# One score product per lent bank, and softmax exponentials handled four heads at a time on GpSimd

## The chip, the cores and the metric

The kernel runs on one core of a Trainium2 chip. The metric is the device time of one execution in microseconds; the median of several runs counts. One further execution is recorded by the hardware profiler; its trace is what the readings below come from. Engine names are those of the profile: PE is TensorE (PEld its weight loads), DVE is VectorE, ACT is ScalarE, POOL is GpSimd, SP is SyncE, which issues most of the transfers.

## The reference

A conditioned transformer block on `x` of shape 2 x 2048 x 512, with 16 heads of 32 and a hidden layer of 2048:

```python
mod = silu(condition) @ Wada + bada
sh_a, sc_a, gt_a, sh_m, sc_m, gt_m = split(mod, 6, axis=1)
xm = layernorm(x, g1, be1) * (1 + sc_a) + sh_a
x = x + gt_a * attention(xm, Wqkv, Wproj, bproj)      # causal, softmax over keys
xm = layernorm(x, g2, be2) * (1 + sc_m) + sh_m
h = gelu(xm @ W1 + b1)                                # exact gelu
x = x + gt_m * (h @ W2 + b2)
```

In `attention`, `scores = q k^T / sqrt(32)`, entries above the diagonal are minus infinity, and the softmax subtracts the largest score of each row.

## The kernel before, in words

The two batch rows go one after the other: projections to queries, keys and values (`Qkv`), attention (`attention_phase`), output projection (`project_phase`), and the next row's projections. The hidden layer for both rows comes last. The dense products use a seven-product scheme for 2 x 2 blocks. Nearly every matmul goes through one helper, so its line is L206 for all of them, and the tiles tell them apart.

Attention is cut into 16 units per batch row: a group `c` of four heads (`HC = 4`) and a block `i` of 512 queries, in the order i = 0, 1, 2, 3 for the first group and 0, 2, 1, 3 for the others. A unit runs steps over tiles of 128 keys: 4 i full steps, then the tile on the diagonal, a step with two tiles (384 and 128 queries wide) and a last one of 256 queries. In a step (`scores_t`) PE writes for each of the four heads the negated row maximum into an `st` bank of PSUM (the fold matmul, `st<-fold,sel`) and adds the transposed scores (`st<-qst,kst`); ACT takes the exponential into a tile `e` (L630); on the last three steps of the unit GpSimd zeroes the masked part of `e` (`affine_select`, L636). Two steps later (`LAG = 2`) PE multiplies `e` by the values (`o<-e,vv`).

The sums of the exponentials are formed in chains of four full steps: GpSimd adds the second tile to the first, the third and the fourth to that (`begin_chain`, `add_to`, L658), and PE reduces the chain over partitions four steps after the last add (`sm<-ee,ones`). The diagonal step's tile joins the last chain; the unit's last steps are summed by PE directly. In the last unit of a batch row VectorE does the adds in place of GpSimd. Tiles rotate: 16 `e` tiles are four steps of four heads, 8 `ee` tiles two chains.

The row maxima of a unit must be known before it begins. `Row` computes them up to three units ahead (`AHEAD = 3`): PE computes scores untransposed (`s<-kst,qst`) into a bank, and VectorE reduces them, a full-width product of 512 keys by a maximum (L500), one on the diagonal by a masked maximum (L495, followed by a read of the accumulator). Products on the diagonal are only 128, 256, 384 or 512 wide; `banks_of` puts two of them into one bank (a pair: 128 with 384, or 256 with 256), all others stand alone. When a unit's list is done, `split` reduces the maxima and splits them into three 16-bit parts (L517 to L521, with the last bank as scratch), and `rows` turns them into the fold operand (L561, L565).

PSUM's eight banks: four `st`, two `s` (`ps_sp`), one `o`, one `sm`. A planner (`count`, `due`) gives each attention step a number of score banks, `n`. With `n` of 3 or more, two of them are computed in `s` after the first two heads' exponentials; after the heads, one takes a borrowed `st` bank (`score(1, st_bank)`), and the fourth takes `s` again:

```python
if n >= 3:
    row.score(1, st_bank)
    row.score(min(n, HC) - 3)
```

`score` takes the list `todo` from its head, in the order of `banks_of`, whether the next entry is a pair or a single. The same function also runs during `Qkv`, between the projections' products, without a borrowed bank. Every instruction of `mm` and `act` keeps its place in the program's order on its engine.

Of the kernel before, what the change touches and what calls it, by code (L numbers as in the profile page):

```python
# [27 lines left out]
def dit_block_kernel(  # L28
# [45 lines left out]
    MTT = MT // P  # L74
    NG = T // MT
    LAG = 2
    E_BUFS = 16
    EE_BUFS = 8
    AHEAD = 3

    const = ctx.enter_context(tc.tile_pool(name="const", bufs=1))
# [213 lines left out]
    class Row:  # L295
# [234 lines left out]
                n += 1  # L530
            return n

        def score(self, n, borrow=None):

            for k in range(n):
                if borrow and k % 2 == 0:
                    s = borrow()  # L540
                else:
                    s = ps_sp.tile([P, QB], F32, tag="s", name="s")
                item = self.todo.pop(0)
                u = item[0]
                if self.mx is None:
                    self.mx = bp.tile(
                        [P, HC * TQ, units[u][1] + 1], F32, tag="mx", name="mx", bufs=3
                    )
                self.bank(*item, s)
                if not self.todo or self.todo[0][0] != u:  # L550
                    self.split(u, self.mx, s)
                    self.mx = None
                    self.at += 1
# [26 lines left out]
    def attention_phase(row):  # L580
        b, vv, kst, qst = row.b, row.vv, row.kst, row.qst
        with pool(f"att{b}") as ap, pool(
# [6 lines left out]
            def scores_t(u, step, n):  # L589

                def st_bank():

                    n_bank[0] += u == len(units) - 1
                    if n_bank[0] % 6 >= HC:
                        return ps_sp.tile([P, QB], F32, tag="s", name="st")
                    return ps_stp.tile([P, QB], F32, tag="st", name="st")

                c, i = units[u]
                tiles = steps_of[u][step]
                q0 = tiles[0][1]
                w = sum(QB - q for _, q in tiles)
                sts, es = [], []  # L610
                for h in range(HC):
                    g = slice(h * HD, (h + 1) * HD)
                    st = st_bank()
                    mm(
                        st[:, :w], sel[g, :], fold[u % 2][g, q0 : q0 + w],
                        start=True, stop=False,
                    )
                    sts.append(st)
                for h in range(HC):
                    at = 0  # L620
                    for j, q in tiles:
                        mm(
                            sts[h][:, at : at + QB - q],
                            kst[c, j // TQ][:, h, j % TQ * P : (j % TQ + 1) * P],
                            qst[u][:, h, q:],
                            start=False, stop=at + QB - q == w,
                        )
                        at += QB - q
                    e = ap.tile([P, QB], F32, tag="e", name="e", bufs=E_BUFS)
                    act(nc.scalar.activation(e[:, :w], sts[h][:, :w], AF.Exp))  # L630
                    if tiles[0][0] >= i * TQ:

                        d = e.rearrange("p (t k) -> p t k", k=P)[:, 0 : TQ : TQ - 1, :]
                        d = d[:, : len(tiles), :]
                        act(
                            nc.gpsimd.affine_select(  # L636
                                d, d, pattern=[[0, len(tiles)], [1, P]],
                                compare_op=ALU.is_ge, fill=0.0,
                                base=0, channel_multiplier=-1,
                            )  # L640
                        )
                    es.append(e)
                    if h < 2 and n >= 3 or h >= HC - n and n < 3:
                        row.score(1)
                if n >= 3:
                    row.score(1, st_bank)
                    row.score(min(n, HC) - 3)
                return es, max(0, n - HC)

            def new_sums():  # L650
                return [
                    ap.tile([P, QB], F32, tag="ee", name="ee", bufs=EE_BUFS)
                    for _ in range(HC)
                ]

            def add(u, h, dst, x, y):
                engine = nc.vector if u == len(units) - 1 else nc.gpsimd
                act(engine.tensor_tensor(dst, x, y, ALU.add))  # L658

            def add_to(u, chain, es):  # L660
                for h in range(HC):
                    add(u, h, chain[h], chain[h], es[h])

            def begin_chain(u, es0, es1):
                chain = new_sums()
                for h in range(HC):
                    add(u, h, chain[h], es0[h], es1[h])
                return chain

            def products(dst, lhs, es, q0, at, first, last):  # L670
                for h in range(HC):
                    mm(
                        dst[h * HD : (h + 1) * HD, q0:], lhs(h),
                        es[h][:, at : at + QB - q0], start=first, stop=last,
                    )

            def finish(u, o, sm):
# [1359 lines left out]
```

## Time and profile before

| | |
|---|---|
| median of 3 runs | 2343.66 us (2343.58 to 2346.75) |
| the profiled execution | 2339.57 us, span 2337.8 us, granted clock 0.997 |
| busy: PE, DVE, ACT, POOL | 2272.5, 1432.3, 1007.9, 1119.2 us |
| attention of the first row, 214 to 748 us | PE 520.4, DVE 358.4, ACT 302.4, POOL 436.5 us busy |
| attention of the second row, 990 to 1518 us | PE 515.7, DVE 354.8, ACT 298.0, POOL 430.9 us busy |

A busy time counts the modelled run of an instruction, and matmuls overlap in the pipeline. A row of a timeline reads: start, length, engine, line, operation, output<-inputs, shapes, how many in a row, and in brackets the idle time of the engine ahead of it with what ended it. A row of the waits reads: who waited for whom, microseconds in all, times, the longest. A row of a group ends in busy time, the mean of one in nanoseconds, and the idle time ahead of the group with what ended it. Line numbers are those of the kernel before.

### The profile page before, as it was taken

What the parts mean: (1) busy time and instruction counts of PE and PEld (TensorE: products, weight loads), DVE (VectorE), ACT (ScalarE), POOL (GpSimd) and SP (SyncE); (2) the same over time, 40 slices, a digit from 0 to 9 for tenths busy, and PEclk for the clock granted to TensorE, in tenths of its full rate; (3) what the DMA queues carried; (4) which work ended last, traced back from release to release, by engine and by line L of the source; (5) the groups of instructions that cost most, each with busy time, mean ns of one, the idle gap of its engine ahead of it and who ended that gap; (6) DMA issues with size and microseconds to landing.
All of it is one profiled execution on the core that took longest, in us unless ns stands there. A gap on an engine that the chain in (4) does not pass through costs nothing.

```text
span 2337.8 us, 34364 instructions
## 1 busy us (share of the span) xinstructions
PE 2272.5 (97%) x12033; PEld 1376.1 (59%) x12033; DVE 1432.3 (61%) x3025; ACT 1007.9 (43%) x1952; POOL 1119.2 (48%) x1261
## 2 busy tenths in 40 slices
PE   7999999999999999999999999999999999999998
PEld 5787445455544588754545554344585486487477
DVE  4677766767657657777576766562473383375356
ACT  4434555555555243355555555603323322332320
POOL 7153997988893692289888898450000000000000
PEclk9999999999999999999999999999999999999999
DMA  9887132231223796622324113263354254353433
GB/s 303 272 277 185 33 86 65 64 83 46 91 100 116 260 307 222 167 60 67 75 64 100 42 42 133 97 229 108 107 176 154 84 176 145 116 162 126 141 120 131
DMA packets 160518, 311.64 MB, mean 133 GB/s; under 512 B 16544, under 2 KB 48844, under 8 KB 158552
## 3 DMA queue, kind: packets, MB, share of 16 engines
q1 hardware_dynamic: 155488, 285.53, 40.5%
q0 software_dynamic: 4480, 23.36, 2.6%
q8 instruction: 95, 1.56, 0.3%
q14 instruction: 79, 0.65, 0.1%
q10 hardware_dynamic: 376, 0.55, 0.1%
HBM read 229.95 MB, written 87.29 MB: 136 GB/s over the span
## 4 chain that ended last, share of the span: by engine, by line
PE 83%; DVE 6%; POOL 6%; issue 2%; DMA 2%; ACT 1%; SPq 0%; DVEq 0%; POOLq 0%; ACTq 0%
PE ps_a L206 24%; PE st L206 15%; PE ps_b L206 12%; PE o L206 9%; PE s L206 7%; PE ps_c L206 6%; POOL ee L658 5%; PE sm L206 4%; PE ps_o L206 3%; DVE junk L495 2%; PE ps_xt L214 1%; DVE mx L500 1%; POOL e L636 1%; ACT e L630 1%; PE ps_o L214 1%
## 5 line engine op out<-in xcount | busy, mean ns | idle before, releaser
L630 ACT ACTIVATE e<-st 128x512 f32<-128x512 f32 (+1 forms) x1152 | 574.5, 578 | 413.6 <-PE st L206 380.0
L500 DVE TENSOR_REDUCE mx<-s 128x1 f32<-128x512 f32 x608 | 406.2, 686 | 223.1 <-PE s L206 221.8
L658 POOL TENSOR_TENSOR ee<-ee,e 128x512 f32<-128x512 f32 x424 | 529.1, 1293 | 3.5 <-ACT e L630 3.3
L206 PE MATMUL st<-qst,kst 128*128 128x512 f32 (+3 forms) x1280 | 410.6, 386 | 0.0
L206 PE MATMUL s<-kst,qst 128*128 128x512 f32 (+3 forms) x994 | 375.3, 402 | 6.0 <-DVE mx L500 3.1
L206 PE MATMUL ps_a<-sum,w 128*128 128x256 f32 (+1 forms) x1088 | 346.6, 454 | 0.0
L206 PE MATMUL o<-e,vv 128*32 128x512 f32 (+3 forms) x2560 | 310.2, 539 | 6.9 <-POOL e L636 6.7
L206 PEld LDWEIGHTS st<-qst,kst 128*128 128x128 f32 x1280 | 227.8, 188 | 117.6 <-issue 88.3
L206 PEld LDWEIGHTS ps_a<-sum,w 128*128 128x128 f32 x1088 | 206.4, 190 | 109.7 <-issue 91.3
L658 POOL TENSOR_TENSOR ee<-e 128x512 f32<-128x512 f32 x168 | 210.3, 1288 | 102.3 <-ACT e L630 100.6
L495 DVE CUSTOM_DVE_ANT_0 junk<-s,causal 128x128 bf16<-128x128 f32 (+3 forms) x386 | 188.5, 488 | 92.4 <-PE s L206 85.0
L206 PEld LDWEIGHTS s<-kst,qst 128*128 128x128 f32 x994 | 185.7, 188 | 55.5 <-DVE mx L500 20.5
L636 POOL TENSOR_SCALAR_AFFINE_SELECT e<-e 128x128 f32<-128x128 f32 (+1 forms) x384 | 123.6, 362 | 73.1 <-ACT e L630 70.8
L206 PEld LDWEIGHTS <-sel 32*128 32x128 bf16 x1152 | 29.5, 91 | 199.7 <-issue 199.7
L1616 DVE TENSOR_TENSOR h<-c,ps_b 128x512 f32<-128x512 f32 x32 | 22.0, 688 | 202.0 <-PE ps_b L206 202.0
L206 PE MATMUL st<-fold,sel 32*128 32x512 bf16 (+1 forms) x1152 | 127.9, 372 | 13.5 <-DVE mx L495 6.4
L206 PEld LDWEIGHTS o<-e,vv 128*32 128x32 f32 x2560 | 65.3, 108 | 112.4 <-issue 72.8
L1790 ACT ACTIVATE h<-h,cols 128x512 f32<-128x512 f32 x96 | 69.3, 722 | 120.5 <-DVE h L1616 120.5
L206 PE MATMUL ps_b<-sum,w 128*128 128x256 f32 (+1 forms) x384 | 120.6, 450 | 0.0
L500 DVE TENSOR_REDUCE mx<-st 128x1 f32<-128x512 f32 x160 | 109.4, 684 | 2.4 <-PE st L206 0.6
L985 POOL TENSOR_TENSOR lo<-lo,hi 128x512 fp32r<-128x512 f32 x32 | 40.7, 1274 | 130.4 <-ACT hi L983 124.1
L206 PE MATMUL st<-kst,qst 128*128 128x512 f32 (+3 forms) x286 | 98.0, 370 | 0.0
(210 smaller groups left out, 3113.9 us busy)
## 6 DMA issues: line engine op xcount, KB each, us to landing
kst<-k SPq DMA_DIRECT2D x128, 256.0 KB
qst<-q SPq DMA_DIRECT2D x128, 256.0 KB
w<-w1d SPq DMA_DIRECT2D x32, 896.0 KB
w<-w2d SPq DMA_DIRECT2D x28, 1024.0 KB
w<-w2d SPq DMA_DIRECT2D x28, 768.0 KB
q<-hi SPq DMA_DIRECT2D x32, 256.0 KB
q<-lo SPq DMA_DIRECT2D x32, 256.0 KB
k<-hi SPq DMA_DIRECT2D x32, 256.0 KB
```

The source lines that it names most:

```text
L206: return tc.keep_in_program_order(nc.tensor.matmul(*args, **kw))
L214: return tc.keep_in_program_order(nc.tensor.transpose(dst, src, ident[:n, :n]))
L495: nc.vector.tensor_tensor_reduce(junk[:, :w], x, causal[:, QB - w :], 1.0, MASKED, ALU.add, ALU.max, m,)
L500: nc.vector.tensor_reduce(m, x, axis=AX.X, op=ALU.max)
L630: act(nc.scalar.activation(e[:, :w], sts[h][:, :w], AF.Exp))
L636: nc.gpsimd.affine_select(d, d, pattern=[[0, len(tiles)], [1, P]], compare_op=ALU.is_ge, fill=0.0, base=0, channel_multiplier=-1,)
L658: act(engine.tensor_tensor(dst, x, y, ALU.add))
L985: engine.tensor_tensor(lo, d, hi.bitcast(F32), ALU.subtract)
L1616: act(nc.vector.tensor_tensor(dst, x, y, ALU.add))
L1790: nc.scalar.activation(d, ps, AF.Gelu, bias=col(r_b1 + half * HF + f, 1))
```

## The change

There are two edits, one on the score products and one on the exponentials.

`score` now looks at the next eight entries of the unit at hand and chooses: a single if there is one, and a pair only where the caller says `late` (the fourth bank of a step) or no single is left. The borrowed bank is used only if a single is there and it is not the unit's last entry; otherwise the product takes an `s` bank.

The exponentials of the four heads of a step go into one tile `e4` of 128 x 4 x 512, one tile per step, four in rotation. ACT still writes it head by head, and PE reads it head by head. GpSimd's select now follows the four exponentials and covers the four heads in one instruction per key tile. GpSimd's adds take 128 x 2048 in one instruction; the last unit's adds on VectorE stay one per head. The chains are one tile of four heads each, two in rotation.

```diff
-    E_BUFS = 16
-    EE_BUFS = 8
+    E_BUFS = 4
+    EE_BUFS = 2
...
-        def score(self, n, borrow=None):
+        def score(self, n, borrow=None, late=False):
             for k in range(n):
-                if borrow and k % 2 == 0:
+                u = self.todo[0][0]
+                ahead = [j for j, item in enumerate(self.todo[:8]) if item[0] == u]
+                pairs = [j for j in ahead if len(self.todo[j][2]) > 1]
+                singles = [j for j in ahead if j not in pairs]
+                lent = borrow and singles and len(ahead) > 1
+                if lent:
                     s = borrow()
                 else:
                     s = ps_sp.tile([P, QB], F32, tag="s", name="s")
-                item = self.todo.pop(0)
-                u = item[0]
+                first = pairs if late else singles
+                item = self.todo.pop((first or [0])[0])
...
+                e4 = ap.tile([P, HC, QB], F32, tag="e", name="e", bufs=E_BUFS)
                 for h in range(HC):
...
-                    e = ap.tile([P, QB], F32, tag="e", name="e", bufs=E_BUFS)
-                    act(nc.scalar.activation(e[:, :w], sts[h][:, :w], AF.Exp))
-                    if tiles[0][0] >= i * TQ:
-                        d = e.rearrange("p (t k) -> p t k", k=P)[:, 0 : TQ : TQ - 1, :]
-                        d = d[:, : len(tiles), :]
+                    act(nc.scalar.activation(e4[:, h, :w], sts[h][:, :w], AF.Exp))
+                    if h < 2 and n >= 3 or h >= HC - n and n < 3:
+                        row.score(1)
+                if tiles[0][0] >= i * TQ:
+                    for n_t in range(len(tiles)):
+                        lo = n_t * (TQ - 1) * P
+                        d = e4[:, :, lo : lo + P]
                         act(
                             nc.gpsimd.affine_select(
-                                d, d, pattern=[[0, len(tiles)], [1, P]],
+                                d, d, pattern=[[0, HC], [1, P]],
...
-                    es.append(e)
-                    if h < 2 and n >= 3 or h >= HC - n and n < 3:
-                        row.score(1)
                 if n >= 3:
                     row.score(1, st_bank)
-                    row.score(min(n, HC) - 3)
-                return es, max(0, n - HC)
+                    row.score(min(n, HC) - 3, late=True)
+                return e4, max(0, n - HC)
...
-            def add(u, h, dst, x, y):
-                engine = nc.vector if u == len(units) - 1 else nc.gpsimd
-                act(engine.tensor_tensor(dst, x, y, ALU.add))
+            def add(u, dst, x, y):
+                if u < len(units) - 1:
+                    act(nc.gpsimd.tensor_tensor(dst, x, y, ALU.add))
+                    return
+                for h in range(HC):
+                    act(nc.vector.tensor_tensor(dst[:, h], x[:, h], y[:, h], ALU.add))
 
             def add_to(u, chain, es):
-                for h in range(HC):
-                    add(u, h, chain[h], chain[h], es[h])
+                add(u, chain, chain, es)
...
                     mm(
                         dst[h * HD : (h + 1) * HD, q0:], lhs(h),
-                        es[h][:, at : at + QB - q0], start=first, stop=last,
+                        es[:, h, at : at + QB - q0], start=first, stop=last,
                     )
```

More of the change, by code (lines that the diff above doesn't have):

```diff
@@ L609, in scores_t @@
                 w = sum(QB - q for _, q in tiles)
-                sts, es = [], []
+                sts = []
                 for h in range(HC):
@@ L641, in scores_t @@
                         )
-                    es.append(e)
-                    if h < 2 and n >= 3 or h >= HC - n and n < 3:
-                        row.score(1)
                 if n >= 3:
                     row.score(1, st_bank)
-                    row.score(min(n, HC) - 3)
-                return es, max(0, n - HC)
[L650 to L654, printed above, removed]
-            def add(u, h, dst, x, y):
-                engine = nc.vector if u == len(units) - 1 else nc.gpsimd
-                act(engine.tensor_tensor(dst, x, y, ALU.add))
+                    row.score(min(n, HC) - 3, late=True)
[6 more added lines that the diff above has]
+                    act(nc.vector.tensor_tensor(dst[:, h], x[:, h], y[:, h], ALU.add))
             def add_to(u, chain, es):
-                for h in range(HC):
-                    add(u, h, chain[h], chain[h], es[h])
+                add(u, chain, chain, es)
             def begin_chain(u, es0, es1):
-                chain = new_sums()
-                for h in range(HC):
-                    add(u, h, chain[h], es0[h], es1[h])
+                chain = ap.tile([P, HC, QB], F32, tag="ee", name="ee", bufs=EE_BUFS)
+                add(u, chain, es0, es1)
                 return chain
```

## The prediction

> **What bounds the kernel now.** I read the page first, then the table of waits, then groups of instructions, and last the timeline at the places the waits pointed to.
>
> ```profile
> span 2337.8 us, 34364 instructions
> PE 2272.5 (97%) x12033; PEld 1376.1 (59%) x12033; DVE 1432.3 (61%) x3025; ACT 1007.9 (43%) x1952; POOL 1119.2 (48%) x1261
> ...
> DVE  4677766767657657777576766562473383375356
> ...
> POOL 7153997988893692289888898450000000000000
> ...
> PE 83%; DVE 6%; POOL 6%; issue 2%; DMA 2%; ACT 1%; SPq 0%; DVEq 0%; POOLq 0%; ACTq 0%
> ```
>
> TensorE is the bound: nothing in this change removes or adds a matmul, so only the time in which PE stands still can be won or lost. The POOL row shows the two attention stretches (slices 5 to 12 and 18 to 25), where GpSimd is at 80 to 90%: the second busiest engine there, and 6% of the chain runs through it and 6% through VectorE. PE's own waits in attention come from these two:
>
> ```profile
> PE o L206 <- POOL e L636: 6.7, 10, 1.2
> PE st L206 <- DVE mx L495: 6.4, 12, 0.8
> PE st L206 <- DVE mhl L521: 6.2, 8, 1.1
> ACT e L630 <- POOL ee L658: 10.9, 8, 1.8
> L206 PE MATMUL s<-kst,qst 128*128 128x512 f32 (+3 forms) x994 | 375.3, 402 | 6.0 <-DVE mx L500 3.1 <-DVE mhl L521 1.8
> ```
>
> The columns are microseconds in all, times, and the longest. I sum these PE rows and correct each from the timeline, because a gap is counted from the modelled end of the matmul before.
>
> **Part 1, the borrowed bank: what goes.** The `st` banks take the fold matmuls of the next step. A bank lent to a score product comes free only when VectorE has read it. One such place with a pair in the lent bank, one where the unit's last product (and with it `split`) sat there, and an undisturbed group of four:
>
> ```profile
> 269.37 0.39 PE L206 MATMUL st<-fold,sel 32*128 32x512 bf16 x3
> 269.49 0.56 DVE L495 CUSTOM_DVE_ANT_0 junk<-st,causal 128x384 bf16<-128x384 f32 x1
> 270.11 0.37 PE L206 MATMUL st<-fold,sel 32*128 32x512 bf16 x1 [0.34 <-DVE mx L495]
> 411.65 0.37 PE L206 MATMUL st<-fold,sel 32*128 32x512 bf16 x1 [0.81 <-DVE mhl L521]
> 336.01 0.39 PE L206 MATMUL st<-fold,sel 32*128 32x512 bf16 x4
> ```
>
> Four folds take 0.39 us together; here three take 0.39 and the fourth 0.37 more after its gap. So each of the 12 + 8 waits costs its gap and 0.37: 6.4 + 12 x 0.37 = 10.8 and 6.2 + 8 x 0.37 = 9.2, together 20.0 us. In the changed program every lent bank holds one single that is not the unit's last, so both rows should go. VectorE's prices say why:
>
> ```profile
> L500 DVE TENSOR_REDUCE mx<-s 128x1 f32<-128x512 f32 x608 | 406.2, 686 | 223.1 <-PE s L206 221.8
> L495 DVE CUSTOM_DVE_ANT_0 junk<-s,causal 128x128 bf16<-128x128 f32 (+3 forms) x386 | 188.5, 488 | 92.4 <-PE s L206 85.0
> L495 DVE DVE_READ_ACCUMULATOR2_ANT mx<- 128x1 f32 x512 | 42.4, 83 | 0.0
> ...
> 362.91 2.29 ACT L630 ACTIVATE e<-st 128x512 f32<-128x512 f32 x4 [2.16 <-PE st L206]
> 376.76 2.06 ACT L630 ACTIVATE e<-st 128x512 f32<-128x512 f32 x4 [1.31 <-PE st L206]
> ```
>
> A single is 0.69 us, a pair is 2 x (0.49 + 0.08) = 1.1. A step scores two products in `s`, then the lent one, then a fourth. With singles first, the lent bank is read out 3 x 0.69 = 2.1 us after VectorE starts on the step's first product. The two exponentials are four steps apart, so a step is about 3.5 us, and PE's next fourth fold comes not quite a step after that product. The pair, now fourth, is read while PE runs the value products.
>
> **What part 1 adds.** Pairs and `split` now always stand in one of the two `s` banks, so PE waits there for VectorE instead, with the step's later `st` products and ACT's exponentials queued behind. At best this is hidden, because the `s` banks are asked for only after the value products and the next folds. At worst all 20 us come back, as waits of `s` instead of `st`. The nearest row is the `s` group's own, 1.8 us for `split` in all, nearer to the lower end; I take the 8 splits that move at 0.5 us, and about as many places where pairs pile up before a unit's end (in the program's order up to three in a row) at 0.25: 6 us. In the projection phases the pairs now stand together too; VectorE has 0.4 us more per slot for six slots in a row. I take nothing, since it is busy in seven tenths of the slices there (3 and 4, 16 and 17), and leave the rest inside those bounds. Part 1 nets 20.0 - 6 = 14 us.
>
> **Part 2, GpSimd by fours: work.** Adds and selects in their present forms, and the one wider add in the trace:
>
> ```profile
> L658 POOL TENSOR_TENSOR ee<-ee,e 128x512 f32<-128x512 f32 x424 | 529.1, 1293 | 3.5 <-ACT e L630 3.3
> L636 POOL TENSOR_SCALAR_AFFINE_SELECT e<-e 128x128 f32<-128x128 f32 x256 | 73.4, 324 | 63.8 <-ACT e L630 63.5
> L636 POOL TENSOR_SCALAR_AFFINE_SELECT e<-e 128x256 f32<-128x256 f32 x128 | 51.7, 439 | 9.3 <-ACT e L630 7.4
> L867 POOL TENSOR_TENSOR wqk<-wqk 128x1024 f32<-128x1024 f32 x1 | 2.4, 2370 | 3.8 <-DVE wqk L867 3.8
> ```
>
> 424 adds busy 529.1 us are 1.25 us each start to start, 5.0 per step of four heads. 512 more columns cost 2370 - 1293 = 1.08 us, so 2048 columns are 2.37 + 2 x 1.08 = 4.5 us (an estimate, called D). Bounds: 2 x 2.37 = 4.74 if the wide one saves nothing more, and 4 x 1.29 = 5.17 if it saves nothing at all. The Trainium skill (GPSIMD Engine Reference, Performance versus the Vector engine) gives 4497 ns for such an add of 2048 columns, a size no run here has shown yet; the sum would be the same. A select gains 0.115 us per 128 columns: 0.44 + 2 x 0.115 = 0.67 for four heads, against 1.0 for four singles; the two-tile step has two, 1.3 against 4 x 0.44 = 1.8.
>
> **Part 2: time.** An add now waits for the fourth exponential, not the first. On GpSimd the adds and selects behind it wait with it; PE's value products two steps on, its row sums, and ACT's first exponential four steps on wait for those. A unit of four query tiles with two chains of adds (i = 2), whose chains start behind the exponentials at 362.91 and 376.76 shown above, before:
>
> ```profile
> 387.75 2.07 ACT L630 ACTIVATE e<-st 128x512 f32<-128x512 f32 x4 [2.15 <-PE st L206]
> 363.59 5.02 POOL L658 TENSOR_TENSOR ee<-e 128x512 f32<-128x512 f32 x4 [6.89 <-ACT e L630]
> 368.55 9.99 POOL L658 TENSOR_TENSOR ee<-ee,e 128x512 f32<-128x512 f32 x8
> 378.47 5.03 POOL L658 TENSOR_TENSOR ee<-e 128x512 f32<-128x512 f32 x4
> 383.43 10.01 POOL L658 TENSOR_TENSOR ee<-ee,e 128x512 f32<-128x512 f32 x8
> 399.32 2.54 POOL L636 TENSOR_SCALAR_AFFINE_SELECT e<-e 128x256 f32<-128x256 f32 x8
> 399.84 2.13 PE L206 MATMUL o<-e,vv 128*32 128x384 f32 x16 [0.32 <-POOL e L636]
> 428.99 1.07 PE L206 MATMUL o<-e,vv 128*32 128x384 f32 x16
> ```
>
> The two-tile select is late, PE waits 0.32 us, and then its 16 products take 2.13 in place of 1.07, paced by the four selects: 1.4 us lost. After: the first add starts at 362.91 + 2.29 = 365.2; three adds end at 378.7; the second chain starts at 376.76 + 2.06 = 378.8 and ends at 392.3; select 393.0, add 397.5, two selects 398.2 and 398.8. PE wants them at 399.84 - 0.32 = 399.5: no wait. ACT's exponential at 387.75 needs the add that would end at 383.3, 4.4 us earlier, so the whole-tile release is covered. The same sum elsewhere:
>
> ```profile
> 325.84 2.06 ACT L630 ACTIVATE e<-st 128x512 f32<-128x512 f32 x4 [1.29 <-PE st L206]
> 347.81 2.13 PE L206 MATMUL o<-e,vv 128*32 128x384 f32 x16 [0.95 <-POOL e L636]
> 675.30 2.07 ACT L630 ACTIVATE e<-st 128x512 f32<-128x512 f32 x4 [2.84 <-PE st L206]
> 697.23 2.13 PE L206 MATMUL o<-e,vv 128*32 128x384 f32 x16 [1.20 <-POOL e L636]
> ```
>
> From 327.9, three adds, a select, an add and two selects end at 327.9 + 4 x 4.5 + 0.67 + 1.3 = 347.9; PE wants its first tile at 346.9 and can have it at 347.2, so about 0.5 to 0.8 is left of 2.0. From 677.4 (one wait for an exponential, 0.3) it ends at 697.6, and 1.1 is left of 2.3. Today the ten gaps and their stretch lose 6.7 + 10 x 1.06 = 17.3 us. Per attention I keep 0.8 + 1.1 and 1.8 for the last unit, where selects stand among other adds: 7.4 in all. Part 2 wins 10 us; bounds 17 if all goes, and, by way of D, a loss (the second rival): at D = 4.8, 365.2 + 7 D + 2.0 reaches the present end of the selects, some 401.
>
> **What is late next.**
>
> ```profile
> 340.40 0.37 PE L206 MATMUL st<-fold,sel 32*128 32x512 bf16 x1 [0.27 <-DVE mx L495]
> 686.60 0.37 PE L206 MATMUL st<-fold,sel 32*128 32x512 bf16 x1 [0.64 <-DVE mhl L521]
> ```
>
> Where a fold wait of part 1 lies after the chain's start in a unit that still waits for GpSimd, PE only arrives earlier at the select. In each attention it is these two places, 0.27 + 0.37 and 0.64 + 0.37: 3.3 us given back.
>
> Sum: 14 + 10 - 3.3 = 21 us. The profiled execution took 2339.57 us, 1.8 beyond its span and 4.1 under the median of the runs, 2343.66; I take the 21 off both: 2318.6 for a profiled execution and **2322.7** for the median.
>
> **A rule that speaks against it.** In the last unit VectorE adds with two SBUF inputs while GpSimd selects, and both are slow there:
>
> ```profile
> 732.88 3.60 POOL L636 TENSOR_SCALAR_AFFINE_SELECT e<-e 128x128 f32<-128x128 f32 x4 [15.70 <-ACT e L630]
> 734.88 3.84 DVE L658 TENSOR_TENSOR ee<-ee,e 128x512 f32<-128x512 f32 x4 [0.18 <-POOL e L636]
> ```
>
> Four selects took 3.60 us here, against 4 x 0.324 = 1.3 at most by the mean. A GpSimd add of 4.5 us meeting such a VectorE instruction would hold it over 3 us longer than one of 1.25. But the long adds end with the unit before, so only selects of 0.67 meet them: no term. The Trainium skill (SBUF — State Buffer, Who interferes with whom) states this as a lock held for the whole instruction by whichever started first; the trace agrees, and by that rule length, not only work, would count wherever the two meet.
>
> **Rivals.**
> *The `s` banks take the waits over* (pairs and `split` in two banks): part 1 nets about 0, part 2 stays at 10 less what is given back, 7: 2337. For it: the `s` row shows that PE waits there already. Against: VectorE idles 221.8 us waiting for PE's `s` products. Chance 0.16.
> *The four-wide add is no cheaper, and starts later by three exponentials (three quarters of 2.06 us).* At D = 5.17 the i = 2 units end at 365.2 + 36.2 + 2.0 = 403.4, 3.4 beyond the 400.0 at which PE needs the second tile (399.5 and half of 1.07), against a loss of 1.4 today: 2 us in eight units; some 1.2 in eight of i = 3 and about 0.7 in eight of i = 1: 30 us lost against 14 won: 2360. It decides from about D = 5.0. For it: only one wide add shows the saving, taken outside attention. Chance 0.11.
> *Nothing of it counts*: PE's gaps are regained by work that VectorE then delays: 2343. Against: the chain runs through PE for 83%. Chance 0.08.
> *All waits vanish*: 20 + 17.3 + 4.9 of the `s` row - 3.3 = 39: 2305. Inside the forecast's upper end, with its chance.
>
> **How the numbers follow.** Forecast 0.65, with all waits gone at its end; the rivals as above. What this kernel's measurement can tell from no change is 0.2%: here 4.7 us. The forecast and most of the first rival (0.13) lie faster: 0.78; the third and the rest of the first give 0.11; slower 0.11. The range runs from 2305 (all waits gone) to 2343 (first and third rival); the slower case is left out.
>
> **What would show it.** Right: the waits of `st` for L495 and L521 gone; adds of 2048 columns at 4.4 to 4.7 us; PE's wait for the select under 3 us; GpSimd's total about 148 x 0.5 + 128 x 0.3 = 112 us lower. Wrong: rows of `s` waiting for VectorE above 12 us, adds over 5 us, or ACT waiting for GpSimd's adds more than the 10.9 us of now.

## The result, and the profile after

The changed kernel takes 2317.41 us (median of 4 runs, 2314.76 to 2318.18) against 2343.62 us before (4 runs, 2339.29 to 2346.75): a ratio of 0.9887, 95% interval 0.9875 to 0.9899, and 26.2 us faster. The forecast was 2322.7 us, 21 us faster. Of all runs reported below, one, at 2367.2 us and a granted clock of 0.948 where the others show 0.994 to 0.999, is left out of its median.

The page of the changed kernel, busy times, the POOL row of the slices, and the shares of the chain:

```profile
span 2313.0 us, 32545 instructions
PE 2252.9 (97%) x12033; PEld 1374.5 (59%) x12033; DVE 1443.8 (62%) x3025; ACT 1006.2 (44%) x1952; POOL 1021.5 (44%) x561
...
POOL 7252986877782692278777879340000000000000
...
PE 84%; POOL 6%; DVE 5%; issue 2%; ACT 1%; DMA 1%; SPq 0%; POOLq 0%; DVEq 0%; ACTq 0%
```

PE has the same 12033 matmuls and 97% of a span that is 24.8 us shorter. GpSimd lost 97.7 us of work, and its share of the chain stayed at 6%. Its groups after (the select is L643 here, the add L656, the exponential L635):

```profile
L656 POOL TENSOR_TENSOR ee<-ee,e 128x2048 f32<-128x2048 f32 x106 | 485.8, 4583 | 16.3 <-ACT e L635 9.0
L643 POOL TENSOR_SCALAR_AFFINE_SELECT e<-e 128x512 f32<-128x512 f32 x128 | 82.1, 663 | 91.8 <-ACT e L635 89.6
```

The waits after, in answer to the rows shown of before:

```profile
PE o L206 <- POOL e L643: 9.3, 8, 2.4
PE st L206 <- DVE mx L495: 1.7, 4, 0.4
PE s L206 <- DVE mx L500: 6.1, 10, 1.2
PE s L206 <- DVE mx L495: 3.8, 9, 1.4
ACT e L635 <- POOL ee L656: 20.8, 15, 1.7
```

The waits of `st` fell from 12.6 us in two rows to 1.7 in one. PE's wait for the select did not fall: 6.7 before, 9.3 now, in eight places instead of ten.

Where the time came from is seen best by units. I cut each attention at the first fold matmul of each unit; the two attentions (208.7 to 744.2 and 980.7 to 1518.3 us before, 210.6 to 735.2 and 971.5 to 1493.1 after) sum to 1073.1 us before and 1046.1 after. That is 27.0 us, the whole gain; all else together moved by 2 us. Below, "attention" is this sum. It is taken from one trace per kernel. Most units that an edit doesn't touch repeat within 0.1 us from kernel to kernel, while the rest of the kernel, outside attention, takes from 1264.4 to 1278.3 us over all the traces of this document; so attention tells small effects better than the medians do.

Where units don't repeat, the granted clock of TensorE differs (PEclk below). Inside the attentions it is 1.00, but for short stretches, nearly all of 3.41 us, in which it is 0.50. The kernel before has one, from 989.9 us, at the head of the second attention; the changed kernel has three, all at waits for masks, 13.7 us together. Two views of its first, then of the same microseconds in the kernel of the fourth experiment below, which has none in attention:

```profile
core 0: us, PE busy (x) PEld busy (x) DVE busy (x) ACT busy (x) POOL busy (x), PEclk, DMA share, GB/s
346.30:349.70 3.40, 3.40 (x27) 2.14 (x19) 0.00 (x0) 0.75 (x2) 1.33 (x3) 0.50 1.06 234
...
346.30:349.70 3.40, 3.28 (x33) 1.85 (x29) 0.20 (x1) 2.43 (x6) 3.40 (x3) 1.00 0.93 196
```

What such a stretch costs can be read where one trace has it in one attention and not in the other: the first unit is 11.74 and 13.32 us in the kernel before, the last unit 47.55 and 49.04 in the seventh experiment. It is some 1.5 us, on top of the wait that it follows, and differences of attention below have to be read with it.

Two places in the changed kernel. At the first (prediction: no wait), GpSimd's selects, then PE's products:

```profile
396.64 1.81 POOL L643 TENSOR_SCALAR_AFFINE_SELECT e<-e 128x512 f32<-128x512 f32 x3
398.36 1.07 PE L206 MATMUL o<-e,vv 128*32 128x384 f32 x16
```

The masks are done as PE arrives, and its 16 products take 1.07 us instead of 2.13. At the second (prediction: 0.5 to 0.8 us left):

```profile
324.01 2.06 ACT L635 ACTIVATE e<-st 128x512 f32<-128x512 f32 x4 [1.35 <-PE st L206]
326.16 4.58 POOL L656 TENSOR_TENSOR ee<-e 128x2048 f32<-128x2048 f32 x1 [0.64 <-ACT e L635]
330.81 9.24 POOL L656 TENSOR_TENSOR ee<-ee,e 128x2048 f32<-128x2048 f32 x2
340.01 0.63 POOL L643 TENSOR_SCALAR_AFFINE_SELECT e<-e 128x512 f32<-128x512 f32 x1
340.72 4.55 POOL L656 TENSOR_TENSOR ee<-ee,e 128x2048 f32<-128x2048 f32 x1
345.23 2.40 POOL L643 TENSOR_SCALAR_AFFINE_SELECT e<-e 128x512 f32<-128x512 f32 x4
345.92 1.64 PE L206 MATMUL o<-e,vv 128*32 128x384 f32 x16 [1.90 <-POOL e L643]
```

PE idles 1.90 us, and the first stretch at half the clock begins here. Just ahead of the masks that it waits for stands an add of 4.55 us, that of the diagonal step's tile, whose sum nobody needs for some time. This is what the experiments turned on.

### The profile page after: what moved, and what is told of

The parts are those of the page before. It is cut to its first block, busy times and chain, and to the rows that moved or that the text cites. A ratio compares the mean times of both kernels' runs of the same rounds, so it can differ in the third digit from the quotient of the medians.

```text
span 2313.0 us, 32545 instructions
## 1 busy us (share of the span) xinstructions
PE 2252.9 (97%) x12033; PEld 1374.5 (59%) x12033; DVE 1443.8 (62%) x3025; ACT 1006.2 (44%) x1952; POOL 1021.5 (44%) x561
## 4 chain that ended last, share of the span: by engine, by line
PE 84%; POOL 6%; DVE 5%; issue 2%; ACT 1%; DMA 1%; SPq 0%; POOLq 0%; DVEq 0%; ACTq 0%
PE ps_a L206 24%; PE st L206 16%; PE ps_b L206 12%; PE o L206 9%; PE s L206 8%; PE ps_c L206 6%; POOL ee L656 4%; PE sm L206 4%; PE ps_o L206 2%; DVE junk L495 2%; PE ps_xt L214 1%; DVE mx L500 1%; ACT e L635 1%; PE ps_o L214 1%; POOL e L643 0%
## 5 line engine op out<-in xcount | busy, mean ns | idle before, releaser
L635 ACT ACTIVATE e<-st 128x512 f32<-128x512 f32 (+1 forms) x1152 | 571.5, 578 | 392.9 <-PE st L206 370.6
L500 DVE TENSOR_REDUCE mx<-s 128x1 f32<-128x512 f32 x578 | 381.6, 686 | 223.0 <-PE s L206 221.9
L656 POOL TENSOR_TENSOR ee<-ee,e 128x2048 f32<-128x2048 f32 x106 | 485.8, 4583 | 16.3 <-ACT e L635 9.0
L206 PE MATMUL s<-kst,qst 128*128 128x512 f32 (+3 forms) x1054 | 381.2, 393 | 10.7 <-DVE mx L500 6.1
L206 PE MATMUL o<-e,vv 128*32 128x512 f32 (+3 forms) x2560 | 293.7, 540 | 9.4 <-POOL e L643 9.3
L495 DVE CUSTOM_DVE_ANT_0 junk<-s,causal 128x128 bf16<-128x128 f32 (+3 forms) x476 | 224.9, 472 | 65.0 <-PE s L206 51.3
L656 POOL TENSOR_TENSOR ee<-e 128x2048 f32<-128x2048 f32 x42 | 192.5, 4583 | 138.9 <-ACT e L635 130.8
L206 PEld LDWEIGHTS s<-kst,qst 128*128 128x128 f32 x1054 | 196.0, 188 | 70.5 <-DVE mx L500 21.7
L500 DVE TENSOR_REDUCE mx<-st 128x1 f32<-128x512 f32 x190 | 129.6, 682 | 0.4
L643 POOL TENSOR_SCALAR_AFFINE_SELECT e<-e 128x512 f32<-128x512 f32 x128 | 82.1, 663 | 91.8 <-ACT e L635 89.6
L206 PE MATMUL st<-fold,sel 32*128 32x512 bf16 (+1 forms) x1152 | 117.5, 374 | 2.8 <-DVE mx L495 1.7
L206 PEld LDWEIGHTS ps_b<-sum,w 128*128 128x128 f32 x384 | 73.0, 190 | 37.2 <-issue 30.6
```

The lines of the kernel that those rows point to most:

```text
L206: return tc.keep_in_program_order(nc.tensor.matmul(*args, **kw))
L495: nc.vector.tensor_tensor_reduce(junk[:, :w], x, causal[:, QB - w :], 1.0, MASKED, ALU.add, ALU.max, m,)
L500: nc.vector.tensor_reduce(m, x, axis=AX.X, op=ALU.max)
L635: act(nc.scalar.activation(e4[:, h, :w], sts[h][:, :w], AF.Exp))
L643: nc.gpsimd.affine_select(d, d, pattern=[[0, HC], [1, P]], compare_op=ALU.is_ge, fill=0.0, base=0, channel_multiplier=-1,)
L656: act(nc.gpsimd.tensor_tensor(dst, x, y, ALU.add))
```

## The experiments

All were timed beside the kernel before. The first four shared their runs of it (median 2343.43), the next four (2343.04) and the last three (2345.46), so medians of different groups compare to about 2 us.

**The two halves by themselves.** First the score order and the bank rule alone (`score` and its calls as in the change, exponentials per head):

```diff
-                    row.score(min(n, HC) - 3)
+                    row.score(min(n, HC) - 3, late=True)   # and score() as changed
```

> The kernel before with the new choice of score products alone; exponentials, selects and adds stay one per head. Theory (two savings that add): the waits of the folds for L495 and L521 (20 us with their stretch) shrink to a few us, about 10 us of waits of the s products replace part of them, and the waits for the selects stay at 6 to 8 us of gaps; some 16 us faster, near 2328. Rival A (only the GpSimd edit counts, PE merely arrives earlier at selects that are as late as before): within 4 us of the kernel before, select gaps over 15 us. Rival B (only the score edit counts): 26 us faster, as the whole change.

Measured: 2336.83 us, ratio 0.9972 (0.996 to 0.9985); 6.6 us faster. Attention 1064.3, 8.8 less. Its waits, and the second place:

```profile
PE o L206 <- POOL e L641: 12.0, 8, 2.4
PE st L206 <- DVE mx L495: 1.7, 4, 0.4
...
348.25 2.99 PE L206 MATMUL o<-e,vv 128*32 128x384 f32 x16 [2.37 <-POOL e L641]
```

The waits of `st` are gone as in the full change, but PE's wait for the select rose from 6.7 to 12.0 us. By units: the one of 56 us ahead of this place lost 3.1 us (56.00 to 52.87), and the short one that holds the place took 2.8 back (12.48 to 15.27). The second attention shows the same (2.3 us there), and so does the head of both last units, where PE meets the masks of the one-chain unit ahead (697 us in the kernel before): 49.72 to 52.34 and 52.02. Each of these four waits is 2.25 to 2.37 us long, and each is followed by 3.41 us at a granted clock of 0.50, the first from 348.98 us.

Then GpSimd by the four alone (the common tile, adds and selects, the order of `score` as before):

```diff
-                    e = ap.tile([P, QB], F32, tag="e", name="e", bufs=E_BUFS)
+                e4 = ap.tile([P, HC, QB], F32, tag="e", name="e", bufs=E_BUFS)   # selects, adds as changed
```

> The kernel before with the exponentials of four heads in one tile and GpSimd's selects and adds by fours; the choice of score products is the old one. Theory (two savings that add): wide adds of 4.6 us, no wait for the selects in the units with two chains, four to six such waits left, the fold waits of 20 us unchanged; some 10 us faster, near 2334. Rival A: 24 us faster. Rival B: within 4 us of the kernel before.

Measured: 2326.94 us, ratio 0.9928 (0.9908 to 0.9948); 16.5 us faster. Attention 1057.7, 15.4 less; waits of `st` unchanged (12.6 us), and PE's wait for the select 4.6 us. So the halves are 8.8 and 15.4 alone and 27.0 together: each is worth more with the other.

**The bank rule without the order.** The list in its old order, a lent bank only for a single that is not the unit's last:

```diff
-                if borrow and k % 2 == 0:
+                if borrow and alone and more:
```

> The kernel before with the old order of score products, but the borrowed bank refused to pairs and to the last product of a unit (those take an s bank in their turn). Separates which bank a pair gets from when it comes. Theory (order matters: a pair in third place in an s bank is asked for too soon): the fold waits go, but the waits of the s products grow well beyond the 10 us of the full change; 4 to 10 us faster than before, near 2336. Rival (the bank alone matters, the order not): as e1_score_only within 3 us.

Measured: 2344.68 us, ratio 1.0001 (0.9989 to 1.0013), attention 1072.9: neither what the theory nor what the rival expected. The waits of `st` vanish, and a row of PE's weight loads grows in their place, from 20.5 us before to:

```profile
PEld s L206 <- DVE mx L500: 47.1, 120, 1.2
```

This is the prediction's first rival, made real by leaving out the order: the products refused by the lent bank queue in the two `s` banks. With the order the same row is 21.7. (The one for L495 is 6.0 before, 9.3 here and 18.1 with the order: pairs do wait there more.)

**The diagonal tile's add, later.** The changed kernel, with that add issued after the masks of the two-tile step:

```diff
                     elif i and n_step == i * TQ:
-                        add_to(u, chain, es)
+                        diag = es
                         sums_of, wait = (chain, False), 2
                     else:
+                        if i and n_step == i * TQ + 1:
+                            add_to(u, chain, diag)
```

> The changed kernel with one move: the add of the diagonal tile to its chain is issued after the selects of the two-tile step, not ahead of them. Theory (what is left of the select waits, 9.3 us of gaps in 8 places, is that one add of 4.6 us standing ahead of the select on GpSimd): the gaps at the first three-chain unit and at the last one-chain unit of each row go, 8 us faster than the changed kernel, near 2309.5. Rival (those places wait for the whole backlog of adds, or the wait moves to ACT and the row sums): less than 3 us.

Measured: 2307.9 us (2306.26 to 2309.3), ratio 0.9845 (0.9826 to 0.9865): 9.5 us under the changed kernel, and the lowest median of all. Attention 1035.7. The second place here:

```profile
342.21 1.81 POOL L643 TENSOR_SCALAR_AFFINE_SELECT e<-e 128x512 f32<-128x512 f32 x3
343.99 4.56 POOL L656 TENSOR_TENSOR ee<-ee,e 128x2048 f32<-128x2048 f32 x1
346.14 1.07 PE L206 MATMUL o<-e,vv 128*32 128x384 f32 x16
```

The masks are done 2.1 us ahead of PE; there is no gap, no stretched products and no stretch at half the clock.

**Which part of "by the four" counts.** My theory was still the prediction's: the wide add. Adds per head in the changed kernel:

```diff
-                if u < len(units) - 1:
-                    act(nc.gpsimd.tensor_tensor(dst, x, y, ALU.add))
-                    return
+                engine = nc.vector if u == len(units) - 1 else nc.gpsimd
                 for h in range(HC):
-                    act(nc.vector.tensor_tensor(dst[:, h], x[:, h], y[:, h], ALU.add))
+                    act(engine.tensor_tensor(dst[:, h], x[:, h], y[:, h], ALU.add))
```

> The kernel after the change, with the common tile of exponentials and the selects by four kept, but GpSimd adding one head at a time (four adds of 512 columns for one of 2048). Theory (the width of the add is what the GpSimd half of the change is worth): four adds take about 5.0 us per set as before the change, against 4.63 us from start to start, the waits of PE for selects that the change removed come back, and the kernel is 8 to 10 us slower than after, near 2326 us; PE's wait for selects above 30 us in the records. Rival (the common tile and the selects by four are what counts): within 3 us of after.

Measured: 2315.64 us, ratio 0.9889 (0.9875 to 0.9904), attention 1045.7: the changed kernel's time. The theory fell, though GpSimd had the work back:

```profile
L657 POOL TENSOR_TENSOR ee<-ee,e 128x512 f32<-128x512 f32 x424 | 528.9, 1287 | 5.0 <-ACT e L635 2.8
...
325.16 2.06 ACT L635 ACTIVATE e<-st 128x512 f32<-128x512 f32 x4 [1.37 <-PE st L206]
326.19 5.00 POOL L657 TENSOR_TENSOR ee<-e 128x512 f32<-128x512 f32 x4
346.69 2.41 POOL L643 TENSOR_SCALAR_AFFINE_SELECT e<-e 128x512 f32<-128x512 f32 x4
```

Selects per head in the changed kernel, adds by four:

```diff
-                if tiles[0][0] >= i * TQ:
-                    for n_t in range(len(tiles)):
-                        d = e4[:, :, lo : lo + P]                        # four heads, one tile
+                    if tiles[0][0] >= i * TQ:
+                        d = e4[:, h] ... [:, 0 : TQ : TQ - 1, :]         # one head, its tiles
```

> The kernel after the change, with adds by four kept, but the masks applied one head at a time as before the change (one select per head over its one or two diagonal tiles). Theory (the adds' width is what counts, the selects only where the products already wait for them): selects cost GpSimd about 1.2 us more per unit with a diagonal and now let the heads go one by one; 2 to 3 us slower than after, near 2320 us. Rival (selects by four are worth as much as the adds): 8 us slower or more.

Measured: 2331.06 us, ratio 0.9943 (0.9924 to 0.9962), attention 1057.0: 13.7 us slower than the changed kernel, 10.9 of it in attention. The rival's 8 us and more. So with the new score order the four corners are, in attention: neither by four 1064.3, adds alone 1057.0, selects alone 1045.7, both 1046.1.

Adds in two halves:

```diff
-                    act(nc.gpsimd.tensor_tensor(dst, x, y, ALU.add))
+                    for h in range(0, HC, 2):
+                        g = slice(h, h + 2)
+                        act(nc.gpsimd.tensor_tensor(dst[:, g], x[:, g], y[:, g], ALU.add))
```

> The kernel after the change with GpSimd's adds cut into two of 1024 columns. Theory: two adds take about 4.7 us per set, start to start, and so within 2 us of after (2316 to 2320 us). Rival (a cost per instruction rules, and half of it comes back): half of the loss of the kernel that adds by head, 4 to 5 us slower than after.

Measured: 2311.49 us, ratio 0.9868 (0.9854 to 0.9882), attention 1038.6: not between the two widths but better than both, by some 6 us against the changed kernel and 7.5 in attention. The second place here:

```profile
328.32 2.07 ACT L635 ACTIVATE e<-st 128x512 f32<-128x512 f32 x4 [1.37 <-PE st L206]
348.90 2.38 POOL L643 TENSOR_SCALAR_AFFINE_SELECT e<-e 128x512 f32<-128x512 f32 x4
349.57 1.07 PE L206 MATMUL o<-e,vv 128*32 128x384 f32 x16 [1.24 <-POOL e L643]
```

Count from the start of the chain's first exponentials to the start of the masks that PE waits for: 345.23 - 324.01 = 21.2 us with adds of 2048 columns, 346.69 - 325.16 = 21.5 with 512, 348.90 - 328.32 = 20.6 with 1024, and 342.21 - 326.21 = 16.0 with the later add (its exponentials start at 326.21). Width buys 0.37 us per step of four heads (5.0 against 4.63 from start to start) and pays for it once: the first add starts 326.16 - 324.01 = 2.15 us after the first exponential does, against 1.03. Over four adds that is about even, and the middle width comes out 0.6 us ahead of the widest. That alone would be small. Over the whole trace PE waits 6.6 us for masks with the middle width against 9.3, and it has one stretch at half the clock where the changed kernel has 13.7 us of them; 2.7 us and, at 1.5 us for every 3.41, some 4.5 (an estimate) make up nearly all of the 7.5. The 4.6 us add ahead of the masks is another size of thing.

**Pairs spread in the `s` slots**, on top of the later add:

```diff
+                left = [len(item[2]) > 1 for item in self.todo if item[0] == u]
+                more = 2 * sum(left) > len(left)
-                first = pairs if late else singles
+                first = pairs if late or more and not lent else singles
```

> The kernel that delays the add of the diagonal tile, with one more edit: in the slots of the s banks a pair is taken as soon as pairs are more than half of what is left of the unit, instead of all pairs at the end. Theory: what is left of PE's waits for s (about 10 us) comes from three pairs in a row at the end of short units, where VectorE cannot keep up; spreading them takes some of it, about 2 us faster than the kernel that only delays the add, near 2306 us. Rival (VectorE's rate over these stretches binds, not the order): no change, within 1 us.

A miss: median of 4 runs 2314.1 us (2305.6 to 2318.3), ratio 0.9876 (0.9853 to 0.9898), and attention 1038.3 us, 2.5 more than without it; neither trace has a stretch at half the clock there. PE's wait of `s` for L495 fell from 3.9 to 2.5 us, but one of `st` for L495 rose from 2.1 to 4.3. In attention the order given by the change was the better one. The median says less: of all traces this one has the longest rest outside attention (where `score` runs too), 1278.3 us.

**The new theory alone.** If the add's place is the cause, one moved line should do in the kernel before what all of "by the four" did. The edit is that of the fourth experiment (in the last unit it moves VectorE's adds as well), in the kernel before, in the kernel with the score order alone, and in the kernel with GpSimd by the four alone.

> The kernel before the change with one edit: the adds of the single diagonal tile to the unit's sums are issued after the masks of the two-tile step that follows, instead of ahead of them; bank order, tiles per head, adds and masks per head all as before. Theory now (what PE waited for was the place of that add, 5 us of GpSimd just ahead of the masks, and not its width): nearly all of the 17 us lost at the masks goes, 13 to 16 us faster than before, near 2329 us, and PE's wait for the select under 2 us. Rival (the masks per head pace the products, four of them in a row, wherever they stand): half or more of it stays, 2335 us or slower.

Measured: 2330.29 us, ratio 0.9938 (0.9926 to 0.995); 15.2 us faster. Attention 1057.4, 15.7 less, against 15.4 for GpSimd by the four; some 1.6 of the 15.7 is the stretch at half the clock at the head of the second attention, which this trace doesn't have. What is left of PE's wait for the select is 2.6 us rather than "under 2", both places in the last units. There the sums are added by VectorE, but on GpSimd another add stands ahead of the masks that PE waits for, L465 of 1.70 us, which already prepares the output projection (the next experiment shows its line):

```profile
PE o L206 <- POOL e L636: 2.6, 2, 1.3
```

> The new order in the borrowed bank, with the add of the diagonal tile after the two-tile masks, and GpSimd by heads as before the change. Theory: with that add out of the way neither the common tile nor masks and adds by four are needed; within 4 us of the kernel that has all of the change and the later add, 2308 to 2312 us, and about 26 us faster than the scoring order alone. Rival (masks by four count for themselves): 2318 us or slower.

Measured: 2309.53 us, ratio 0.9854 (0.9839 to 0.9868), 27.3 us under the score order alone (2336.83). Attention 1040.3. Against the kernel that has everything (1035.7) the difference, 4.6 us, lies in the two last units: 49.66 and 49.71 us here, 47.44 in both there. Two views of the first of them, GpSimd's masks by head here and then, in the kernel of the fourth experiment, by four:

```profile
716.93 4.21 POOL L641 TENSOR_SCALAR_AFFINE_SELECT e<-e 128x128 f32<-128x128 f32 x4 [15.70 <-ACT e L635]
721.11 1.70 POOL L465 TENSOR_TENSOR kst<-kst,bgate 128x512 f32<-128x512 f32 x1
719.52 3.83 DVE L663 TENSOR_TENSOR ee<-ee,e 128x512 f32<-128x512 f32 x4 [0.19 <-POOL e L641]
723.68 2.04 PE L206 MATMUL o<-e,vv 128*32 128x384 f32 x11 [1.26 <-POOL e L641]
```

```profile
721.04 1.48 POOL L643 TENSOR_SCALAR_AFFINE_SELECT e<-e 128x512 f32<-128x512 f32 x1 [17.12 <-ACT e L635]
722.49 1.27 POOL L465 TENSOR_TENSOR kst<-kst,bgate 128x512 f32<-128x512 f32 x1
722.55 5.52 DVE L659 TENSOR_TENSOR ee<-ee,e 128x512 f32<-128x512 f32 x4 [0.53 <-POOL e L643]
725.90 0.43 PE L206 MATMUL o<-e,vv 128*32 128x128 f32 x8 [0.19 <-POOL e L643]
```

Beside VectorE four masks take 4.21 us, one over four heads 1.48. The two don't start alike: the first mask by head follows the first exponential, the wide one the fourth. Counted from the start of the first exponential (716.26 and 718.90 us) the masks are done after 4.9 and 3.6 us. Next on GpSimd comes L465, and only then the masks that PE waits for here; that this add could be moved too wasn't tried.

> GpSimd by the four with the later add, but the order in the borrowed bank as before the change. Theory (what the scoring order wins is given back at the masks as long as GpSimd is late there): with the masks out of the way it is worth the predicted 14 us, so this kernel is about 14 us slower than the one that has both, near 2322 us. Rival (the order is worth only what it showed alone, 7 to 9 us): near 2316 us.

Measured: 2324.81 us, ratio 0.9912 (0.99 to 0.9925), attention 1055.1: 16.9 us slower by the medians than the kernel that has the order too, 19.4 in attention. All corners, attention in us, and in brackets the number of stretches of 3.41 us at half the clock in it (the one of 6.83 counts as two):

| | old order | new order | the order is worth |
|---|---|---|---|
| by heads | 1073.1 (1) | 1064.3 (4) | 8.8 |
| by four | 1057.7 (1) | 1046.1 (4; the change) | 11.6 |
| by heads, add later | 1057.4 (0) | 1040.3 (0) | 17.1 |
| by four, add later | 1055.1 (1) | 1035.7 (0) | 19.4 |

The less PE waits for masks, the more the order of the scores is worth. More than half of that growth goes with the clock: with 1.5 us taken off for each stretch, an estimate, the last column reads 13.3, 16.1, 17.1 and 17.9. And once the add is later, "by the four" is worth 2.3 (old order) to 4.6 us (new), where it was 15.4 and 18.2; less the stretch in one of the traces, the 2.3 is nearer 3.8.

## Why the prediction was right, point by point

The time came out inside the range, and with the mechanisms in part as described. That the sum lay only 5 us off is in part luck: part 1, less what is given back, was put at 10.7 us and measures 8.8 alone; part 2 was put at 10 and measures 15.4; together they are 2.8 us more than their sum, for which the prediction has no term.

- **The bound.** Right in the main: 27.0 us of attention were won with the same matmuls. But PE's standing still isn't all that can be won: a long wait here costs a stretch at half the clock as well, some 1.5 us, and the prediction has nothing for it.
- **Part 1, what goes.** Right: the rows of `st` for L521 and for the pairs went, and the place at 269 us now runs its four folds in 0.40 us together.
- **Part 1, what is added.** Right in size, by luck in what it is made of: PE's rows of `s` rose from 4.9 us to 10.5 (6.1 + 3.8 + 0.6 for `split`), by 5.6 where 6 were taken. Of the 6, 4 were put on the splits, but their row fell, from 1.8 to 0.6; what rose is the waits for L500, from 3.1 to 6.1, and for L495, from none to 3.8. The rows of the weight loads rose more (L500, L495 and L521 from 31.7 us together to 42.1); what of that costs PE time they don't say. The first rival's threshold, 12, was not reached; the third experiment shows that it is what the bank rule brings without the order.
- **Part 1, net 14.** Right only as a middle: 8.8 alone, 19.4 with nothing waiting behind it, or 17.9 without the stretch at half the clock. That it can reach this, more than 20.0 less the 5.6, is not explained by the rows of waits; some 3.5 us stay open.
- **"Given back 3.3": the term that was mis-sized.** The two places per attention were the right ones, the price was not. It was taken as the fold wait that stands between the chain's start and the select. With the order alone the gap at the second place went from 0.95 to 2.37 us and the 16 products from 2.13 to 2.99: 2.3 us where 0.64 was put. Counted from the chain's first exponentials, PE arrived 1.0 us earlier, and the masks came 0.4 later, because GpSimd, its work unchanged and PE quicker, was still adding for the chain before. Over the two places of both attentions 10.0 us were given back where 3.3 were put (2.8 and 2.3 at the first of them, 2.6 and 2.3 at the other, at the head of the last unit), and that is most of 19.4 less 8.8. Of the 10.0, the waits themselves are 5.2: they grew from 0.95, 1.20, 0.65 and 1.20 us to 2.37, 2.26, 2.35 and 2.25. The other half goes with the clock: with the order alone a stretch at half the clock follows each of these four waits, before the change none.
- **Part 2, the work.** D = 4.5 us: 4.583 measured, 4.63 from start to start. The Trainium skill's 4497 ns (GPSIMD Engine Reference, Performance versus the Vector engine) is 2% under this trace's 4583. Select 0.67: 0.663. GpSimd's total fell by 97.7 us for 112: adds went from 739.4 to 678.3 in place of the 74 taken.
- **Part 2, 10 us won.** Low: 15.4 alone. No wait is left at the i = 2 units, as predicted, and the six short units behind those of the later groups (i = 1) are 1.0 to 1.6 us shorter each by this half alone.
- **Part 2, the reason: the step that failed.** The sum was made with D as its driver, from 5.0 to 4.5 per step. The fifth experiment puts the 5.0 back and loses nothing. The two terms of that sum, shorter steps and a later start, were both there and nearly cancel over four adds. What was left over is in the selects (which of their differences counts how much was not taken apart): 1.81 us for three of them where eight took 2.54 (the place at 399 us before, 396 after), one release for all four heads, and in the last unit masks done 1.3 us sooner after the first exponential. At the i = 2 units of the two middle groups either half is nearly enough: the first short unit behind them takes 27.16 us with the adds alone (sixth experiment) and 26.98 with the selects alone, against 28.09 with neither; in the last group it is 24.02 and 23.31, against 24.40 with neither and 22.71 with both.
- **The second rival** (a wide add that is no cheaper loses 30 us from about D = 5.0) wasn't tried as it stood, since the wide add is cheaper. Its driver, though, is weaker than its price says: by head D is 5.0 and the chain starts early.
- **The sign "PE's wait for the select under 3 us"** came out wrong, 9.3. What the prediction called "PE wants" were times of the trace before; PE, quicker by part 1, came earlier; with part 2 alone the row is 4.6. It had looked at what stands ahead of the masks on GpSimd and counted the diagonal tile's add as a term of 4.5 us, without asking whether it must stand there. The later add takes the row away, and with it the stretches at half the clock.
- **The sign "ACT waits for GpSimd's adds more than 10.9 us"** came (20.8) without meaning what it was to mean: these gaps are 1.3 us, and beside them stand gaps of the same 1.3 us that end with PE's `st`. The add was the last to come by the profile, not late. In the fastest kernel the row is 25.6.
- **"No term" for VectorE beside GpSimd in the last unit.** Not so: with the masks by four the last unit is 2.2 us shorter than by head, as the tenth experiment shows. The rule named there (the Trainium skill, SBUF — State Buffer, Who interferes with whom: a lock held for the whole instruction) would fit: four short masks can meet VectorE four times, a wide one once. It was applied to the long adds alone. But the trace doesn't show the count at work so plainly: in the tenth experiment the four masks took 2.56, 0.29, 0.73 and 0.73 us, most of it in the one that was released while VectorE still had a row of instructions to run. That this is where the 2.2 us come from is argued, not shown; L465 differs too, 1.70 us against 1.27.

## What to carry to other kernels

Where the bound engine meets an in-order engine that paces it, what the bound engine saves upstream can be lost at that meeting; price an edit there with the pacing engine's time, not with the wait that it removes. Look at the granted clock beside each longer wait of TensorE: the wait may cost more than its length. Look first at what stands ahead of the awaited instruction in the pacing engine's queue, and whether it is needed yet: one moved add was worth about as much as making all of that engine's instructions wider. Width has two sides, fewer instructions and a later start, and a middle width can beat both ends, as it did here in one run.

## What the runs showed of the hardware

After a wait of TensorE for masks, the granted clock fell to 0.50 for 3.41 us in some cases, and 6.83 in one, beginning at most 0.5 us ahead of the wait's end and at most 1.6 us after it. Over all traces of this document it did so in none of the 13 such waits of 0.9 to 1.5 us, in 7 of 12 between 1.6 and 2.24 us, and in all 8 of 2.25 us and more. What decides between two waits of nearly one length (2.14 us without, 2.16 with, in the third experiment) is not shown. Four traces also have a stretch at the head of the second attention, just behind a wait of 1.07 or 1.08 us for VectorE; the other traces have that wait and no such stretch.

Beside VectorE instructions on two SBUF tiles, a select over 512 columns took 1.48 us in one place and 0.84 in another, against 0.66 by the mean, and one over 128 columns 2.56, against 0.32. That one ended 0.15 us after an unbroken row of VectorE's had ended (719.49 and 719.34 us; in the kernel before 734.85 and 734.70). Four VectorE adds took up to 5.52 us, against 2.49: VectorE is slowed there too, and not GpSimd alone. A GpSimd add takes from start to start 1.25 us for 512 columns, 2.35 for 1024 and 4.63 for 2048: nearly in proportion, so that the widest saves 7%.
